# A channel-attention and convolution block of 16 images on one core: the depthwise sums kept in PSUM, the centre tap merged on GpSimd, the LayerNorm tiles copied whole and scaled on GpSimd, a ring of pixel rows, and a new order of the work

## The chip, the cores and the metric

One core of a Trainium2 chip runs the whole program; the other cores are idle. The metric is the device time of one execution in microseconds (us), and of several executions the median. The engines are TensorE (PE, with its weight loads as PEld), VectorE (DVE), ScalarE (ACT), GpSimd (POOL) and SyncE (SP), and 16 DMA engines serve the core. GpSimd issues here the DMAs that add into their target; SyncE issues the plain loads and stores.

## What is computed

The input x is 16 images of 128 channels and 96 by 96 pixels, all fp32. The reference, cut to what matters:

```python
xn1 = _layernorm(x_hwc)                      # over the 128 channels of a pixel
q, k, v = xn1 @ wq.T, xn1 @ wk.T, xn1 @ wv.T # 8 heads of 16 channels
attn = softmax(l2norm(q) @ l2norm(k).T * scale)   # 16 x 16 per head: over channels
x = x + (attn @ v) @ wp.T
xn2 = _layernorm(x_hwc)
h1 = w_in @ xn2                              # 1x1 conv, 128 -> 512 channels
h2 = depthwise 3x3 conv of h1, zero padding  # 512 channels
x = x + w_out @ gelu(h2)                     # 1x1 conv, 512 -> 128 channels
```

The attention is over channels, so it comes down to one 128 by 128 matrix for each image, which the kernel gets from the Gram matrix of the normalised pixels.

## The kernel before

An image is 8 bands of 12 rows (1152 pixels), and a band is 3 units of 4 rows (384 pixels). Channels lie on the 128 partitions. The 512 hidden channels are 4 chunks of 128. The program treats 128 bands, and for each band 4 chunks.

**Normalisation** (`norm`, lines 555 to 754) is done twice for each image, as a (ahead of the attention) and b (behind it). Groups of 4 tiles of 128 pixels are transposed by TensorE into a PSUM bank (`forth`, line 614), so that pixels lie on the partitions. VectorE takes the sums of two tiles at a time (`stats`, 621), GpSimd adds epsilon and raises to the power -1/2 (`variance` 628, `power` 632), VectorE makes the shift for b (636), and ScalarE writes each tile of 128 by 128 scaled, and for b also shifted, into an SBUF buffer zT (668, 672): 4 instructions for a group. In the first image VectorE takes half of these. TensorE forms the Gram matrix from zT (682, a only), and transposes back (719); ScalarE writes the result into the pixel buffers xn (723, 725), each of which holds 24 rows of an image and one more row at either side, so that a row at a border is written twice (729).

**Attention** (757) is a chain of small steps over all engines, once an image. Its result is a matrix that `mix` (571) applies to the normalised pixels; ScalarE writes the product into an x buffer (580), and a DMA of GpSimd's queue adds the image to it (583).

**The convolution** of a chunk goes one of two ways.

- *Job* (`conv_job`, 886): TensorE makes the hidden rows (906), ScalarE copies them from PSUM to SBUF (911; 902 copies the two rows shared with the next band). The nine taps are then summed over shifted windows of these rows. The weights are divided by the centre's, so that the centre is added unscaled. The first tap on VectorE reads two windows in SBUF and writes the sum h3 in SBUF (924); each further one reads a window and h3 and writes h3 (930). Two taps (3 and 5; a third one in chunk 1) are products of ScalarE (919); a DMA of GpSimd's queue adds one product to another (`pr<-pr`, 940), and one more adds the sum to h3 (`h<-pr`, 940). ScalarE takes the gelu in place (944). The windows cut at the image's border have 1140, 1056 or 1045 elements in place of 1152.
- *By matmuls* (`by_matmuls`, 975): chunk 3 of some bands goes directly from xn to the depthwise sum, by nine accumulating matmuls for each unit (990), with the gelu out of PSUM (1000). `PE_BANDS` and `PE_OF` choose these bands: 61 of the 128, which leaves 451 jobs, the last of them without products.

`ffn_out` (1008) multiplies the four gelu results with w_out into PSUM (1017), VectorE adds that to x (1024), and SyncE stores the band.

**PSUM** has 8 banks: 2 for `forth`, 1 for `back`, 1 for the Gram matrix and the attention, and 4 (h) that hidden rows, `mix`, convolutions and outputs share.

**Order.** No engine chooses its work on the chip. `Plan` (58) is a list scheduler that runs while the program is built: each operation has an engine, an assumed duration, what it reads and writes, and a place, which is its turn plus an offset from the table `AT`. The plan goes through an assumed time, lets each engine take the ready operation of the lowest place, and hands out buffers. What comes out is one order, and each engine then works through its own part of it strictly in that order, with semaphores between engines.

Of the kernel before, what the change touches and what calls it, by code (L numbers as in the profile page):

```python
# [20 lines left out]
PE_BANDS = (0, 2, 4, 6, 8, 10, 12)  # L21
PE_OF = 15
# [8 lines left out]
THIRDS = ((1, 1, (0,)),)  # L31
PART, Z_PARTS = 24, 6
QT, QB = 4, 1
H_BANKS = 4
X1_BUFS, XB_BUFS, PR_BUFS, H3_BUFS, ZT_BUFS = 2, 6, 5, 10, 3
IN_TURN = ("tr", "h3", "pr", "xb", "x1")
AT = dict(
    load_w=-20.2, weights=13.4, zeros=-68.05, load_a=-147.85, forth_a=-13.65, stats_a=-60.15, variance_a=574.05,
    power_a=353.05, scaled_a=35.3, gram=0.3, back_a=-44.8, place_a=177.6, attention=-146.15, mix=-16.25,
    residual=204, mixed=-47.8, add_x=-331.2, forth_b=-11.5, stats_b=-104.75, variance_b=68.55, power_b=-326.9,  # L40
    shift_b=-87.05, scaled_b=162.15, back_b=-5.95, place_b=38.15, halo=227.9, hidden=2.75, kept=-114.4,
    products=153.15, add_last=-10.05, tap=4.7, add_first=-147.85, gelu=241.95, conv=3.5, conv_gelu=5.8, out=7,
    add=-70.85, store=278.2, mix_0=-75.3, residual_0=369.55, mixed_0=-142.3, add_x_0=-398.7, gram_0=126.2,
    forth_a_0=-269.2, forth_b_0=-14.9, stats_a_0=-113.85, stats_b_0=-48.05, scaled_a_0=100.95, scaled_b_0=286.6,
    back_a_0=-115.65, back_b_0=-181.55, place_a_0=-352.8, place_b_0=-9.75, shift_b_0=-101.75, late=-3.55,
)
STEP = dict(scaled=0.3, hidden=0.1, products=0.5, tap=0.166, conv=1.6, conv_tap=0.03, out=0.8, out_part=0.05)
# [6 lines left out]
T_POWER = 1000  # L54
T_ADD, T_MOVE = 3060, 1640


class Plan:
# [7 lines left out]
    def __init__(self, **pools):  # L66
        self.free = {p: list(range(n)) for p, n in pools.items()}
        self.slot = {}
        self.ops, self.writer, self.readers, self.users = [], {}, {}, {}
        self.dma = 0.0  # L70
        self.two = 0.0
# [31 lines left out]
    def order(self):  # L103
# [14 lines left out]
        for k, o in enumerate(ops):  # L118
            queues.setdefault(o[0], [])
            idle[o[0]] = True  # L120
            for t in o[5]:
                queue_of[t[0]].append((o[2], k))
# [19 lines left out]
        def dispatch(engine, time):  # L142
# [22 lines left out]
            elif engine == "POOL":  # L165
                rest = self.two - time
                ns, result = (ns, result) if rest <= 0 else (rest + ns - 143, rest + result - 143)
                own = result
            if o[9]:
                self.two = time + ns + 35  # L170
# [42 lines left out]
def tile_restormer_block(  # L213
# [35 lines left out]
    UPP, PARTS = PART // UR, H // PART  # L249
    D = C // HEADS  # L250
    assert PE_CHUNK == NCH - 1 and BR * W >= 8 * P and QT % 2 == 0 and NU * TPU % (QB * QT) == 0 and C == P and UT % P == 0 and H % PART == 0 and PART % BR == 0 and NCH == 4
# [7 lines left out]
    p_tr = ctx.enter_context(tc.tile_pool(name="p_tr", bufs=2, space=PSUM))  # L259
    p_bk = ctx.enter_context(tc.tile_pool(name="p_bk", bufs=1, space=PSUM))  # L260
# [4 lines left out]
    banks = [p_h.tile([P, 4 * P], F32, name=f"h_{k}") for k in range(H_BANKS)]  # L265


    ident = const.tile([P, P], F32, name="ident")
    make_identity(nc, ident)
    blocks = const.tile([P, P], F32, name="blocks")  # L270
# [37 lines left out]
    xns = [pad.tile([P, (PART + 2) * WP + 2], F32, name=f"xn{k}") for k in range(Z_PARTS)]  # L308
# [11 lines left out]

    zT_bufs = [h1p.tile([P, QT, P + 1], F32, name=f"zT_{k}") for k in range(ZT_BUFS)]
# [15 lines left out]
    def part_of(i, r):  # L337

        return (i * PARTS + r // PART) % Z_PARTS, r % PART

    def interior(i, u):
        k, r = part_of(i, u * UR)
        return window(xns[k], r + 1, UR, 1)

    def z_unit(i, u):
        k, r = part_of(i, u * UR)
        return ("z", k, r // UR)
# [754 lines left out]
```

## Time and profile before

| | |
|---|---|
| median of 3 runs | 4148.34 us |
| the runs | 4149.0, 4148.34, 4136.15 us |
| span of the profiled execution (first to last instruction) | 4137.5 us |
| instructions | 52025 |
| moved by DMA | 833.50 MB, mean 201 GB/s |
| HBM read, written | 148.26 MB, 75.50 MB |
| matmuls from xn in `by_matmuls` (two instructions each) | 3294 instructions |
| taps on VectorE | 451 first, 2129 further |
| products on ScalarE | 1028 |

The profile is of one execution. It gives the span but no time of its own beside it, so what lies around the span is seen only against the timed runs: their median is 10.8 us above it. A row of the groups reads: line, engine and operation, the tiles written and read, their shapes, the count, and then the busy time in us, the mean duration of one in ns, and the time that the engine idled just ahead of it. Each fp32 matmul is two instructions, each transpose one. Instructions of one engine overlap a little at their ends, so a mean duration is longer than the time from one start to the next; that time is read from a timeline. The busy share of an engine counts the overlap once.

### The profile page before, as it was taken

How to read it: one execution, taken by the hardware profiler on the slowest of the kernel's cores; microseconds unless marked ns; L12 is line 12 of the kernel's file. 1: busy time of each engine (PE TensorE's matmuls, PEld its weight loads, DVE VectorE, ACT ScalarE, POOL GpSimd, SP SyncE). 2: the span in 40 equal slices, each digit the busy share in tenths (PEclk: the TensorE clock that was granted, in tenths of full speed). 3: DMA queues.
4: the chain of work that ended last, by engine and by line, in shares of the span. 5: the costliest groups of instructions: out<-in, count | busy, mean ns of one | idle time of the engine just before them, and what ended most of it. 6: DMA issues, size and time to landing. Idle time of an engine off the chain costs nothing.

```text
span 4137.5 us, 52025 instructions
## 1 busy us (share of the span) xinstructions
PE 4064.3 (98%) x17217; PEld 2630.9 (64%) x17217; DVE 4048.7 (98%) x4706; ACT 3674.7 (89%) x6993; POOL 2538.1 (61%) x2357
## 2 busy tenths in 40 slices
PE   8999999999999999999999999999999999999999
PEld 6666666666666666666666666666666666666555
DVE  6999999999999999999999999999999999999998
ACT  5899989999889998999899989999889989999886
POOL 4657656566665757657566665666646666566442
PEclk9999999999999999999999999999999999999999
DMA  2999999999999999999999999999999999999998
GB/s 87 193 195 213 205 213 204 206 217 199 211 203 204 209 198 209 216 200 207 199 216 197 209 201 206 213 207 204 200 198 211 205 213 209 194 208 205 192 195 187
DMA packets 205372, 833.50 MB, mean 201 GB/s; under 512 B 23728, under 2 KB 25136, under 8 KB 205104
## 3 DMA queue, kind: packets, MB, share of 16 engines
q0 software_dynamic: 165600, 678.37, 84.6%
q1 hardware_dynamic: 38256, 151.73, 9.8%
q8 instruction: 136, 2.23, 0.2%
q14 instruction: 132, 1.08, 0.1%
q10 hardware_dynamic: 1248, 0.09, 0.0%
HBM read 148.26 MB, written 75.50 MB: 54 GB/s over the span
## 4 chain that ended last, share of the span: by engine, by line
PE 40%; DVE 10%; ACT 5%; DMA 3%; issue 2%; POOL 1%; POOLq 0%; ACTq 0%; DVEq 0%
PE h L990 11%; PE h L1017 10%; PE h L906 8%; DVE h L930 7%; PE g L682 2%; PE h L571 2%; DMA h<-pr 2%; DVE h L924 2%; PE pB_a L719 1%; ACT pr L919 1%; PE pT_b L614 1%; PE pT_a L614 1%; PE pB_b L719 1%; DMA pr<-pr 1%; ACT h L911 1%
## 5 line engine op out<-in xcount | busy, mean ns | idle before, releaser
L930 DVE SCALAR_TENSOR_TENSOR h<-h,ratio,h 128x1140 f32<-128x1140 f32 (+3 forms) x2129 | 2890.9, 1378 | 5.0
L919 ACT ACTIVATE pr<-h,ratio 128x1152 f32<-128x1152 f32 x1028 | 1337.2, 1307 | 98.7 <-DMA h<-pr 63.1
L990 PE MATMUL h<-xn,comp 128*128 128x380 f32 (+1 forms) x3294 | 1160.5, 483 | 3.6 <-ACT h L911 1.5
L1017 PE MATMUL h<-h,woutT 128*128 128x384 f32 x3072 | 1129.9, 487 | 11.4 <-ACT h L944 4.7
L906 PE MATMUL h<-xn,winT 128*128 128x384 f32 (+2 forms) x2706 | 1055.9, 494 | 8.0 <-ACT h L911 6.1
L940 POOL DMA_DIRECT2D pr<-pr x578 | 558.3, 977 | 478.3 <-ACT pr L919 312.0
L990 PEld LDWEIGHTS h<-xn,comp 128*128 128x128 f32 x3294 | 596.9, 190 | 348.8 <-issue 6.5
L911 ACT COPY h<-h 128x384 f32<-128x384 f32 (+2 forms) x1353 | 670.0, 525 | 142.0 <-PE h L906 110.8
L1017 PEld LDWEIGHTS h<-h,woutT 128*128 128x128 f32 x3072 | 555.7, 190 | 347.1 <-issue 25.0
L906 PEld LDWEIGHTS h<-xn,winT 128*128 128x128 f32 x2706 | 485.6, 190 | 302.4 <-issue 35.9
L940 POOL DMA_DIRECT2D h<-pr x450 | 447.6, 998 | 361.5 <-PE h L906 73.8
L924 DVE SCALAR_TENSOR_TENSOR h<-h,ratio 128x1152 f32<-128x1152 f32 x451 | 633.8, 1408 | 5.0 <-ACT h L911 2.8
L944 ACT ACTIVATE h<-h 128x1152 f32<-128x1152 f32 x453 | 549.4, 1216 | 14.9 <-DMA h<-pr 8.9
L632 POOL TENSOR_TENSOR rstd_a<-ve_a,mhalf 128x4 f32<-128x4 f32 x288 | 535.3, 1859 | 13.0 <-POOL ve_a L628 0.2
L628 POOL TENSOR_SCALAR ve_a<-st_a 128x4 f32<-128x4 f32 x288 | 347.3, 1206 | 286.9 <-DVE st_a L621 263.2
L632 POOL TENSOR_TENSOR rstd_b<-ve_b,mhalf 128x4 f32<-128x4 f32 x288 | 516.5, 1794 | 10.6
L672 ACT ACTIVATE zT<-pT_b,nb_b,rstd_b 128x128 f32<-128x128 f32 x1132 | 434.3, 494 | 47.4 <-DVE nb_b L636 40.6
L628 POOL TENSOR_SCALAR ve_b<-st_b 128x4 f32<-128x4 f32 x288 | 285.5, 996 | 301.9 <-DVE st_b L621 285.5
L668 ACT ACTIVATE zT<-pT_a,rstd_a 128x128 f32<-128x128 f32 x1080 | 320.3, 422 | 18.9 <-POOL rstd_a L632 17.7
L682 PEld LDWEIGHTS g<-zT 128*128 128x128 f32 x2304 | 295.1, 192 | 45.0 <-issue 4.4
L682 PE MATMUL g<-zT 128*128 128x129 f32 x2304 | 305.1, 275 | 0.0
L571 PE MATMUL h<-xn,mwT 128*128 128x384 f32 x768 | 287.1, 490 | 6.6 <-ACT h L911 3.2
(171 smaller groups left out, 3585.7 us busy)
## 6 DMA issues: line engine op xcount, KB each, us to landing
pr<-pr POOLq DMA_DIRECT2D x578, 576.0 KB, 7.5
h<-pr POOLq DMA_DIRECT2D x450, 576.0 KB, 7.7
x<-in_x_dram SPq DMA_DIRECT2D x128, 576.0 KB, 6.8
out_dram<-x SPq DMA_DIRECT2D x127, 576.0 KB, 6.3
x<-in_x_dram POOLq DMA_DIRECT2D x122, 576.0 KB, 7.2
out_dram<-x SPq DMA_DIRECT2D x3, 192.0 KB, 1.9
weights<-in_L_conv_w_in_dram SPq DMA_DIRECT2D x1, 256.0 KB, 2.9
weights<-in_L_conv_w_out_dram SPq DMA_DIRECT2D x1, 256.0 KB, 3.0
```

The lines of the kernel that those rows point to most:

```text
L628: nc.gpsimd.tensor_scalar(ve, d["mv"][:, :, 2], 1.0 / C, EPS, ALU.mult, ALU.add)
L632: nc.gpsimd.tensor_tensor(rstd, d["ve"], mhalf, ALU.pow)
L682: nc.tensor.matmul(grams[i][:, : P + 1], lhsT=zt[:, :P], rhs=zt, start=(q == 0 and k == 0), stop=(q == NU * TPU // QT - 1 and k == QT - 1),)
L906: nc.tensor.matmul(rows(ph), lhsT=winT[:, n, :], rhs=window(xn, r0 + r, e - r, 1), start=True, stop=True)
L911: nc.scalar.copy(window(h1_, r, e - r, 1), rows(d.pop(("ph", r))))
L919: nc.scalar.activation(to, shifted(t), AF.Copy, scale=ratio[:, n, t : t + 1])
L924: nc.vector.scalar_tensor_tensor(h3, shifted(t), ratio[:, n, t : t + 1], shifted(UNIT), ALU.mult, ALU.add)
L930: nc.vector.scalar_tensor_tensor(to, shifted(t)[:, lo:hi, cut], ratio[:, n, t : t + 1], to, ALU.mult, ALU.add)
L940: nc.gpsimd.dma_start(out=to, in_=d["pr", t], accum_op=ALU.add)
L944: nc.scalar.activation(h3, h3, AF.Gelu)
L990: nc.tensor.matmul(d["pc"][:, lo:hi, cut], lhsT=comp[:, t, :], rhs=window(xn, r0 + dy, UR, dx)[:, lo:hi, cut], start=(t == order[0]), stop ...
L1017: nc.tensor.matmul(rows(d["po"]), lhsT=woutT[:, n, :], rhs=h3s[g, n][:, s * UR : (s + 1) * UR, :], start=(k == 0), stop=(k == NCH - 1),)
```

## The change

- **Taps.** Every job (but the last) now has three products on ScalarE, taps 3, 5 and a third. GpSimd adds the first of them to the centre's window into one buffer `merged` (both operands in SBUF). VectorE has 5 taps: the first reads a window and `merged`, the middle three read a window and the sum, the last reads a window and the sum and writes h3. The sum `acc` is one buffer in PSUM (3 banks), the same for every job. The other two products are added by DMA, one to the other and then to h3.
- **Bands by matmuls:** 41 in place of 61, so 471 jobs.
- **LayerNorm.** ScalarE copies the PSUM bank of 4 tiles in one instruction to zT; VectorE takes the sums from zT in SBUF; GpSimd scales the four tiles in place with one instruction whose second operand is the 4 columns of the power, broadcast. For b, TensorE multiplies with a centring matrix (identity minus 1/128) in place of a transpose, so the shift goes away. In the first image VectorE scales half.
- **Pixels** lie in one ring of 132 rows, in place of 6 buffers of 24, so a row is written twice only at the ring's seam.
- **PSUM:** `forth` and `back` lose their banks and share the 4 banks h; 3 banks are `acc`.
- **Order:** all offsets of `AT` are new, a `RANK` is added that changes the order but not the turn for a buffer, the plan's idea of VectorE and GpSimd holding each other up is new, and the numbers of buffers change (x 6 to 5, products 5 to 7, h3 10 to 8, zT 3 to 7).

```diff
-PE_BANDS = (0, 2, 4, 6, 8, 10, 12)
-PE_OF = 15
+PE_BANDS = (0, 3, 6, 10, 13, 16, 20, 23, 26)
+PE_OF = 30
-THIRDS = ((1, 1, (0,)),)
+THIRDS = ((0, 1, (0,)), (1, 1, (0,)), (2, 1, (0,)), (3, 1, (0,)))
...
+    acc_banks = p_acc.tile([P, ACC_BANKS * 4 * P], F32, name="acc")
+    acc = acc_banks[:, : BR * W].rearrange("p (r w) -> p r w", w=W)
+    centre = const.tile([P, P], F32, name="centre")
+    nc.vector.tensor_scalar(centre, ident, -1.0 / C, None, ALU.add)
...
-                    nc.tensor.transpose(d["pT", q][:, k, :], xt[:, j * P : (j + 1) * P], ident)
+                    if second:
+                        nc.tensor.matmul(
+                            d["pT", q][:, k, :], lhsT=xt[:, j * P : (j + 1) * P], rhs=centre, start=True, stop=True
+                        )
+                    else:
+                        nc.tensor.transpose(d["pT", q][:, k, :], xt[:, j * P : (j + 1) * P], ident)
...
+                nc.vector.bn_stats(d["st"][:, j, :], zT(qs[h])[:, k : k + 2, :P].rearrange("p t c -> p c t"))
...
+            def copied(q):
+                nc.scalar.copy(zT(q)[:, :, :P], d["pT", q])
+
+            def scaled(engine, q, ks):
+                z = zT(q)[:, ks[0] : ks[-1] + 1, :P]
+                t = (q - qs[0]) * QT
+                rstd = d["rstd"][:, t + ks[0] : t + ks[-1] + 1]
+                engine.tensor_tensor(z, z, rstd.unsqueeze(2).to_broadcast([P, len(ks), P]), ALU.mult)
...
+        def merge():
+            nc.gpsimd.tensor_tensor(merged, d["pr", dma_taps[0]], shifted(UNIT), ALU.add)
...
         def tap(t):
-            h3 = h3_of(g, n)
-            if t == left[0]:
-                nc.vector.scalar_tensor_tensor(
-                    h3, shifted(t), ratio[:, n, t : t + 1], shifted(UNIT), ALU.mult, ALU.add
-                )
+            if t in (left[0], left[-1]):
+                to = h3_of(g, n) if t == left[-1] else acc
+                also = acc if t == left[-1] else merged if dma_taps else shifted(UNIT)
+                nc.vector.scalar_tensor_tensor(to, shifted(t), ratio[:, n, t : t + 1], also, ALU.mult, ALU.add)
                 return
             lo, hi, cut = inside(t, b * BR, BR)
-            to = h3[:, lo:hi, cut]
+            to = acc[:, lo:hi, cut]
             nc.vector.scalar_tensor_tensor(
                 to, shifted(t)[:, lo:hi, cut], ratio[:, n, t : t + 1], to, ALU.mult, ALU.add
             )
...
         def add_products(t):
-            to = d["pr", dma_taps[0]] if t != dma_taps[0] else h3_of(g, n)
-            nc.gpsimd.dma_start(out=to, in_=d["pr", t], accum_op=ALU.add)
+            nc.gpsimd.dma_start(out=d["pr", dma_taps[1]], in_=d["pr", t], accum_op=ALU.add)
+
+        def add_h3():
+            nc.gpsimd.dma_start(out=h3_of(g, n), in_=d["pr", dma_taps[1]], accum_op=ALU.add)
```

More of the change, by code (lines that the diff above doesn't have):

```diff
@@ L164, in dispatch @@
                 result = own = self.dma + result - time
[L165 to L170, printed above, removed]
+            elif engine == "POOL" and o[9]:
+                rest = max(0, self.two - time)
+                ns, result, own = rest + ns, rest + result, rest + own
+                self.held = time + ns
+            if o[9] and engine == "DVE":
+                rest = max(0, self.held - time)
+                ns, result, own = rest + ns, rest + result, rest + own
+                self.two = time + ns
+                self.lost += rest
             push(time + own, "own", k)
@@ L693, in pixels @@
-            op("POOL", T_VARIANCE, at("variance" + ab, s), variance, [], [bt], T_VARIANCE + 33 + SLACK + 200)
-            op("POOL", T_POWER, at("power" + ab, s), power, [], [bt], T_POWER + 33 + SLACK + 700)
-            if second:
-                dve(80, at("shift" + ab, s, i), shift, [], [bt])
-            for h, (q, tr) in enumerate(zip(qs, trs)):
+                zt = zt_of(q)
+                both = [(*zt, j) for j in range(2)]
+                if apart and q % 2 == 0:
+                    four = [(*zt_of(k), j) for k in (q, q + 1) for j in range(2)]
+                    op("POOL", 200, at("zeros", s), lambda q=q: zT(q), [], four, 300)
```

239 lines of the change are left out of this document (129 added, 110 removed).

## The prediction

> **What bounds the kernel now.** First the page's head: the span, the busy shares, and the two DMA queues that carry the traffic (packets, MB, share of 16 engines).
>
> ```profile
> span 4137.5 us, 52025 instructions
> PE 4064.3 (98%) x17217; PEld 2630.9 (64%) x17217; DVE 4048.7 (98%) x4706; ACT 3674.7 (89%) x6993; POOL 2538.1 (61%) x2357
> ...
> q0 software_dynamic: 165600, 678.37, 84.6%
> q1 hardware_dynamic: 38256, 151.73, 9.8%
> ...
> PE 40%; DVE 10%; ACT 5%; DMA 3%; issue 2%; POOL 1%; POOLq 0%; ACTq 0%; DVEq 0%
> ```
>
> Two engines are busy 98% of the time and the DMA engines 94%, so no single one can be sped up alone. The stages tell whether that holds in the middle. A row has the stretch, its length, then for PE, PEld, DVE, ACT and POOL the busy time and (x) the instructions, then the clock, the DMA share and GB/s.
>
> ```profile
> 200.00:4000.00 3800.00, 3753.53 (x15841) 2422.87 (x15840) 3757.68 (x4288) 3442.62 (x6545) 2389.97 (x2154) 1.00 0.97 205
> ```
>
> From 200 to 4000 us VectorE idles for 42 us of 3800, TensorE for about as long, at a full clock. The chain of waits has TensorE with 40% and VectorE with 10% of the span, in pieces of a few us. So the time follows VectorE and TensorE together: it goes down by what the one of them that loses less work loses, as long as ScalarE (89%), GpSimd and the DMA engines don't come up to it. I therefore count each engine's work before and after.
>
> **VectorE, taps.**
>
> ```profile
> L930 DVE SCALAR_TENSOR_TENSOR h<-h,ratio,h 128x1140 f32<-128x1140 f32 x1548 | 2129.6, 1392 | 3.5
> L924 DVE SCALAR_TENSOR_TENSOR h<-h,ratio 128x1152 f32<-128x1152 f32 x451 | 633.8, 1408 | 5.0 <-ACT h L911 2.8 <-PE h L1017 1.5 <-PE pB_a L719 0.6
> L930 DVE SCALAR_TENSOR_TENSOR h<-h,ratio,h 128x1045 f32<-128x1045 f32 x226 | 290.0, 1292 | 0.2
> L636 DVE SCALAR_TENSOR_TENSOR nb_b<-st_b,rstd_b 128x4 f32<-128x4 f32 x288 | 43.4, 151 | 10.0 <-POOL rstd_b L632 9.9
> ```
>
> The means hold overlap, so I take the time from start to start from a timeline (start, duration, engine, what).
>
> ```profile
> 2038.37 0.15 DVE L636 SCALAR_TENSOR_TENSOR nb_b<-st_b,rstd_b 128x4 f32<-128x4 f32 x1
> 2038.44 5.35 DVE L930 SCALAR_TENSOR_TENSOR h<-h,ratio,h 128x1140 f32<-128x1140 f32 x4
> ...
> 2047.67 1.40 DVE L924 SCALAR_TENSOR_TENSOR h<-h,ratio 128x1152 f32<-128x1152 f32 x1
> 2049.11 2.86 DVE L930 SCALAR_TENSOR_TENSOR h<-h,ratio,h 128x1140 f32<-128x1140 f32 x2
> 2051.89 1.41 DVE L924 SCALAR_TENSOR_TENSOR h<-h,ratio 128x1152 f32<-128x1152 f32 x1
> ```
>
> Four taps in 5.35 us, the last of 1.39 whole, give (5.35 - 1.39)/3 = 1.32 us a tap; these are of two jobs in turn. The pair at 2049.11 takes 2.86, so 1.46 from start to start, and it starts 1.44 behind the tap at 2047.67: a tap that waits for the one before it costs 0.11 to 0.14 us more. I take 0.13.
>
> Before there are 451 + 2129 = 2580 taps. After, 471 jobs have 5 each, the last 8: 2358. So 222 fewer, by 1.32: **-293 us**. The 288 shifts of L636 go (0.07 each from start to start, 2038.37 to 2038.44): -20 us.
>
> Now the price of the new form. A tap's sum lies in PSUM. The nearest rows:
>
> ```profile
> L577 DVE SCALAR_TENSOR_TENSOR x<-h,d,x 128x384 f32<-128x384 f32 x18 | 10.8, 612 | 5.1 <-PE h L571 4.9
> L811 DVE TENSOR_TENSOR wide<-g,wqkT 128x256 f32<-128x256 f32 x15 | 6.2, 413 | 4.5 <-ACT wide L807 4.4
> L857 DVE TENSOR_TENSOR em<-e,blocks 128x128 f32<-128x128 f32 x16 | 4.5, 282 | 0.0
> L621 DVE BATCH_NORM_STATS2 st_b<-pT_b 128x6 f32<-128x256 f32 x566 | 234.8, 420 | 8.4 <-PE pT_b L614 7.8
> L1024 DVE TENSOR_TENSOR x<-h,x 128x384 f32<-128x384 f32 x384 | 209.5, 545 | 10.6 <-PE h L1017 10.3
> ```
>
> The taps of 1140 and 1045 elements differ by 100 ns, 1.05 an element. Without that, what is left is 612 - 403 = 209 ns for a form with three operands that reads PSUM (h), 1392 - 1197 = 195 for the tap in SBUF; 413 - 269 = 144 with PSUM (g) against 282 - 134 = 148 without. So reading PSUM costs nothing; that VectorE writes PSUM no row shows. Bounds: half of the 144 ns more or less, 0.07 us by 4 writing taps in 470 jobs, +-132 us. I take 0, as reading does. The statistics, read from SBUF in place of PSUM, I take as unchanged for the same reason.
>
> [...]
>
> There is one sum buffer for all jobs, so each tap waits for the one before it, across jobs too: 470 x 5 = 2350 gaps of 0.13. What hides them is other VectorE work put between: 1152 statistics (566 in the row above) and 384 adds. If every one falls in a gap, 814 stay open (106 us); if none, all do (305). The order is made by a plan that takes any ready work in a gap, so I take 950: **+124 us**.
>
> The first tap still reads two SBUF windows. GpSimd rows show what that means.
>
> ```profile
> 2045.87 0.19 POOL L628 TENSOR_SCALAR ve_b<-st_b 128x4 f32<-128x4 f32 x1 [0.68 <-DVE st_b L621]
> 2047.84 1.29 POOL L628 TENSOR_SCALAR ve_a<-st_a 128x4 f32<-128x4 f32 x1 [1.78 <-DVE st_a L621]
> 2049.09 1.03 POOL L632 TENSOR_TENSOR rstd_b<-ve_b,mhalf 128x4 f32<-128x4 f32 x1
> ```
>
> The read at 2045.87, beside statistics out of PSUM, took 0.19. The same at 2047.84 took 1.29 and ended at 2049.13, just behind the tap of 2047.67 (to 2049.07). So a tap with two SBUF windows holds a GpSimd read up; VectorE work with one does not. That VectorE is held by GpSimd no row shows. A merge can't meet a first tap, since `merged` is one buffer that the tap must have read. A scaling can: 576 of about 1.07 us (below) are 16% of the span, half of one is left on the mean: 470 x 0.16 x 0.5 = 35 us; bounds 0 and three times that, with power and variance counted. I take **+35**.
>
> VectorE: -293 - 20 + 124 + 35 = **-154 us**, 4137.5 to 3983.
>
> **TensorE.**
>
> ```profile
> 2037.67 4.65 PE L990 MATMUL h<-xn,comp 128*128 128x384 f32 x14
> ...
> 2042.16 0.60 PE L614 MATMUL pT_b<-ident,x 128*128 128x128 f32 x4
> ...
> 2070.68 1.05 PE L682 MATMUL g<-zT 128*128 128x129 f32 x8
> ```
>
> From start to start: (4.65 - 0.49)/13 = 0.320 for 384 columns, (0.60 - 0.27)/3 = 0.109 for a transpose, (1.05 - 0.27)/7 = 0.111 for each half of a matmul of 129 columns with its own weights. Bands by matmuls go from 61 to 41, so 1080 of 3294 instructions go: -346. Hidden rows of 20 more jobs, counted over the bands: 170 more of 384 columns, 60 fewer of 480 (0.40 in proportion), 10 more of 288 (0.24): +32. The 1152 transposes of b become matmuls: 0.222 - 0.109 each, +130. **-184 us**, to 3953, if it idles as long as today (4137.5 - 4064.3 = 73). This is below VectorE's 3983, so VectorE is late last, by 30 us.
>
> **ScalarE.**
>
> ```profile
> 2038.66 0.47 ACT L911 COPY h<-h 128x384 f32<-128x384 f32 x1
> 2039.02 1.26 ACT L919 ACTIVATE pr<-h,ratio 128x1152 f32<-128x1152 f32 x1
> 2040.18 1.50 ACT L672 ACTIVATE zT<-pT_b,nb_b,rstd_b 128x128 f32<-128x128 f32 x4
> 2041.55 1.28 ACT L919 ACTIVATE pr<-h,ratio 128x1152 f32<-128x1152 f32 x1
> 2042.69 1.16 ACT L668 ACTIVATE zT<-pT_a,rstd_a 128x128 f32<-128x128 f32 x4
> 2043.69 1.22 ACT L944 ACTIVATE h<-h 128x1152 f32<-128x1152 f32 x1
> 2044.75 0.64 ACT L723 ACTIVATE xn<-pB_b,b 128x384 f32<-128x384 f32 x1
> ```
>
> ```profile
> L919 ACT ACTIVATE pr<-h,ratio 128x1152 f32<-128x1152 f32 x1028 | 1337.2, 1307 | 98.7 <-DMA h<-pr 63.1 <-DMA pr<-pr 33.9 <-ACT xn L725 0.2
> L672 ACT ACTIVATE zT<-pT_b,nb_b,rstd_b 128x128 f32<-128x128 f32 x1132 | 434.3, 494 | 47.4 <-DVE nb_b L636 40.6 <-PE g L682 2.2 <-PE pB_a L719 1.3
> L668 ACT ACTIVATE zT<-pT_a,rstd_a 128x128 f32<-128x128 f32 x1080 | 320.3, 422 | 18.9 <-POOL rstd_a L632 17.7 <-PE g L682 0.7 <-issue 0.2
> ```
>
> From start to start: a hidden copy 0.36, a product 1.16, four scalings 1.37 (b) and 1.00 (a), a gelu 1.06. The 2258 scalings (those of the first image apart, 285 and 279 groups) go: -670. 576 copies of 512 elements come, at 0.47 (128 more elements than a hidden copy, at no more than a product's 1.16/1152 each, make it at most 0.49): +271. Products go from 1028 to 1410: +443. The 20 more gelus are +21, 60 unit gelus of the bands by matmuls go (-24), hidden copies +19, border rows -21, shared rows +10. **+49 us**, 3724: 93% of 3983. It doesn't become the bound, but it has to serve more PSUM banks in time.
>
> **DMA.**
>
> ```profile
> pr<-pr POOLq DMA_DIRECT2D x578, 576.0 KB, 7.5
> h<-pr POOLq DMA_DIRECT2D x450, 576.0 KB, 7.7
> ...
> x<-in_x_dram POOLq DMA_DIRECT2D x122, 576.0 KB, 7.2
> ```
>
> 1028 adds become 470 x 2 = 940, and adds of x 122 become 123: 1063 for 1150, each 0.846 x 4137.5/1150 = 3.04 us of all engines. -264 us: from 94% to 91% of the shorter span.
>
> **GpSimd** gets the work that the others lose.
>
> ```profile
> masks.py:383 POOL TENSOR_SCALAR_AFFINE_SELECT blocks<-blocks 128x128 f32<-128x128 f32 x1 | 0.3, 344 | 0.1
> masks.py:197 POOL MEMSET ident<- 128x128 f32 x1 | 0.2, 204 | 0.3 <-POOLq L1091 0.3
> L648 POOL MEMSET zT<- 128x4 f32 x18 | 0.7, 104 | 0.0
> ...
> L940 POOL DMA_DIRECT2D pr<-pr x578 | 558.3, 977 | 478.3 <-ACT pr L919 312.0 <-DMA pr<-pr 27.4 <-ACT h L911 26.9
> L632 POOL TENSOR_TENSOR rstd_a<-ve_a,mhalf 128x4 f32<-128x4 f32 x288 | 535.3, 1859 | 13.0 <-POOL ve_a L628 0.2
> L628 POOL TENSOR_SCALAR ve_a<-st_a 128x4 f32<-128x4 f32 x288 | 347.3, 1206 | 286.9 <-DVE st_a L621 263.2 <-DVE nb_b L636 16.5 <-DMA pr<-pr 2.5
> ```
>
> No row shows a large two-operand operation. Two memsets of 128 and 4 columns give 0.8 ns an element and 0.1 us fixed; 344 ns for the select give at most 2.7 ns an element, and 1.9 without the fixed part. So a merge of 1152 costs 1.0 to 3.1 us, and I take 1.9 ns: 2.3, with some for the second operand 2.4 us; a scaling of 512 1.07 (0.5 to 1.4). 470 x 2.4 = 1128, 576 x 1.07 = 616, powers 576 x 1.03 and variances 576 x 0.19 = 703, DMA issues 1063 x 0.98 = 1042, the rest 30: 3519 us. The first taps, 470 x 1.33, fill 16% of the span, so of the 1728 reads other than merges 16% meet one and wait 0.7: 194. Together **3713, or 93%** of 3983. Today's 2538 hold nearly 1000 of such waiting (means of 1.86 and 1.2 us where 1.03 and 0.19 are free of it), so there is room, but little is left.
>
> [...] A merge waits for a product of ScalarE and for the first tap of the job ahead; queued behind it are the DMA adds, powers and scalings, and for these wait the gelus, the transposes back and, a job later, VectorE. [...]
>
> **The sum.** VectorE's 3983 in the profiled execution's terms; the median of the timed runs lies 10.8 us above that span: 3983 + 11 = 3994, say **3990** (-3.8%).
>
> **The rivals.**
>
> - *GpSimd is the bound* (slower). At 2.7 ns an element merges take 3.1 us, scalings 1.38: 1775 for the rest + 1457 + 795 + 194 = 4221, with the 89 us that VectorE idles today 4310, + 11 = **4320**. It decides from merges of 2.86 us. For it: VectorE waits for a merge in each job, from a queue that runs in order. Against: the price that the rows suggest is below. 0.14.
> - *The gaps stay open*: all 2350, +181 us on the forecast: **4174**; slower than before from 2150 of them. Against: 1536 pieces of other work. 0.07.
> - *Four banks are too few.* Banks h take 2304 groups of work now, 4 x 4137/2304 = 7.2 us each; after 3625 groups, 4.4 us each, of which (3953 - 73)/3625 = 1.07 is TensorE's writing.
>
> ```profile
> L719 PEld LDWEIGHTS pB_a<-ident,zT 128*128 128x128 f32 x1152 | 144.2, 141 | 110.4 <-issue 42.1 <-ACT xn L725 19.1 <-ACT zT L668 9.2
> ```
>
>   This weight load, behind the one bank of `back`, waits 19.1 us in 384 groups for ScalarE, 0.05 each. If all 3625 groups did: +180 on TensorE's 3953, 4133 + 11 = **4144**. Against: tiles now leave a bank by one copy. 0.08.
> - *Writing PSUM is dear*, at the upper bound: **4122**. [...]
> - *The port isn't freed*: the change's middle taps hold GpSimd's reads up all the same, so 3113 us of taps and 1744 of merges and scalings exclude each other: 4857 + 89 + 11, about **4960**. Against: the read at 2045.87. 0.04.
>
> **How the numbers follow.** The forecast has 0.62, from 3890 (TensorE's 3953, less the 73 us that it idles today, and 11) to 4100. The range 3890 to 4180 takes in the open gaps and the banks, and leaves out GpSimd as the bound (0.14), the port (0.04) and a little below. The measurement can tell 0.3%, 12 us, from no change: faster are the forecast, the dear PSUM and part of the banks, 0.70; within 0.3% the rest of the banks and of the forecast's tail, 0.08; slower 0.22.
>
> **What would show it.** Right: about 1880 taps on `acc` with 1.32 us from start to start, or 1.45 behind their like; merges of 2.2 to 2.6 us beside them; GpSimd 90 to 95% busy, VectorE 95% or more, ScalarE and TensorE 93 to 97%. Wrong: first taps that wait for `merged`; VectorE idle over 150 us; taps of 1.5 us or of several; weight loads that wait for copies; a DMA share above 95%.

## The result, and the profile after

The changed kernel takes **4101.73 us** (median of 4 runs, 4094.66 to 4103.59) where the kernel before took 4142.24 beside it: ratio 0.9905, 95% interval 0.9884 to 0.9926. That is faster by 0.95%, a quarter of the 3.8% forecast (3990), and inside the range. The head of the page after, in the rows shown of before:

```profile
span 4100.5 us, 52124 instructions
PE 3932.9 (96%) x17409; PEld 2600.1 (63%) x17409; DVE 3893.5 (95%) x4170; ACT 3716.6 (91%) x5675; POOL 3492.2 (85%) x3320
...
q0 software_dynamic: 153072, 627.05, 80.3%
q1 hardware_dynamic: 38256, 151.73, 10.2%
...
PE 30%; DVE 25%; POOL 16%; DMA 12%; ACT 10%; issue 7%; POOLq 0%; DVEq 0%; ACTq 0%
```

VectorE's work fell by 155 us (4048.7 to 3893.5) and TensorE's by 131, as the forecast had it for VectorE to within a microsecond. The span fell by 37. The rest is idle time: VectorE 207 us in place of 89, TensorE 168 in place of 73. And the chain of waits is of another kind: TensorE's 40% has become 30%, while VectorE went from 10% to 25%, GpSimd from 1% to 16%, DMA from 3% to 12% and ScalarE from 5% to 10%. (The chain before covers 61% of its span, the one after all of it. Of the part that is covered, TensorE had 66%, VectorE 16%, ScalarE 8%, DMA 5% and GpSimd 2%, so the move from TensorE to GpSimd and DMA is there all the same.) The same stretch as before, in the same columns:

```profile
200.00:4000.00 3800.00, 3653.52 (x16050) 2401.49 (x16050) 3657.55 (x3840) 3520.26 (x5361) 3295.34 (x3061) 0.99 0.93 195
```

Both leading engines idle for 142 to 147 us of 3800 in the middle too, where it was about 42 to 46; it is no matter of start or end. Groups of VectorE after (count, busy, mean ns, idle ahead of them and for what):

```profile
L960 DVE SCALAR_TENSOR_TENSOR acc<-h,ratio,acc 128x1140 f32<-128x1140 f32 x1062 | 1487.0, 1400 | 14.1
L956 DVE SCALAR_TENSOR_TENSOR acc<-h,ratio,merged 128x1152 f32<-128x1152 f32 x470 | 736.9, 1568 | 37.6 <-POOL merged L947 21.8 <-DVE h L956 0.5
L956 DVE SCALAR_TENSOR_TENSOR h<-h,ratio,acc 128x1152 f32<-128x1152 f32 x471 | 661.6, 1405 | 8.4 <-PE h L1065 1.7
L665 DVE BATCH_NORM_STATS2 st_b<-zT 128x6 f32<-128x256 f32 x576 | 244.8, 427 | 31.9 <-ACT zT L690 31.8
L1072 DVE TENSOR_TENSOR x<-h,x 128x384 f32<-128x384 f32 x384 | 211.6, 551 | 53.1 <-PE h L1065 47.8 <-ACT pr L944 2.3 <-ACT xn L745 0.8
```

The middle taps on PSUM cost 1400 ns (1392 in SBUF before) and the last ones 1405: reading and writing PSUM costs next to nothing, 8 ns. Only the first tap, which reads two SBUF windows, is long on the mean, 1568. The idle time is spread over results that come late from everywhere: from TensorE (47.8), ScalarE (31.8) and GpSimd (21.8). Two rows of a timeline show the tap's price. The first tap at 1072.73 takes 1.99 us:

```profile
1071.22 1.41 DVE L956 SCALAR_TENSOR_TENSOR h<-h,ratio,acc 128x1152 f32<-128x1152 f32 x1
1072.73 1.99 DVE L956 SCALAR_TENSOR_TENSOR acc<-h,ratio,merged 128x1152 f32<-128x1152 f32 x1
```

And GpSimd in the same stretch (a span there starts while the instruction ahead of it still runs: the scalings' at 1070.80, with the issue ahead of them ending at 1072.40):

```profile
1067.80 3.76 POOL L947 TENSOR_TENSOR merged<-pr,h 128x1152 f32<-128x1152 f32 x1
1070.18 2.22 POOL L969 DMA_DIRECT2D pr<-pr  x1
1070.80 4.79 POOL L696 TENSOR_TENSOR zT<-zT,rstd_a 128x512 f32<-128x512 f32 x2
1072.80 3.77 POOL L674 TENSOR_TENSOR rstd_a<-ve_a,mhalf 128x4 f32<-128x4 f32 x1
```

So the ends are what can be compared: the merge ends at 1071.56, the DMA issue at 1072.40, the two scalings at 1075.59, the power at 1076.57. From the end of the issue the two scalings take 3.19 us, where two of the shortest (1.04, at 1361.81) would take 2.08. They lose about 1.1 us, just when the first tap runs (1072.73 to 1074.72), and the tap takes 1.99 in place of 1.41. The power ends 0.98 behind the scalings and loses nothing; its 3.77 is a wait in the queue. So in this stretch a tap with two operands in SBUF and GpSimd's scalings, which read SBUF, hold each other up, in both directions: 0.58 us lost by the tap, about 1.1 by the scalings.

Last, ScalarE's waits for sums that the DMA engines form, before and after (us in total, times, longest):

```profile
ACT pr L919 <- DMA h<-pr: 63.1, 65, 3.3
ACT pr L919 <- DMA pr<-pr: 33.9, 35, 2.9
ACT h L944 <- DMA h<-pr: 8.9, 7, 2.4
```

```profile
ACT h L976 <- DMA h<-pr: 54.5, 56, 3.9
ACT pr L944 <- DMA h<-pr: 33.4, 22, 4.3
ACT pr L944 <- DMA pr<-pr: 32.6, 35, 2.8
```

The gelu (L944 before, L976 after) waits for its sum for 54.5 us where it was 8.9.

### The profile page after: what moved, and what is told of

Its sections match the earlier page's. It is cut to its first block, busy times and chain, and to the rows that moved or that the text cites. A ratio compares the mean times of both kernels' runs of the same rounds, so it can differ in the third digit from the quotient of the medians.

```text
span 4100.5 us, 52124 instructions
## 1 busy us (share of the span) xinstructions
PE 3932.9 (96%) x17409; PEld 2600.1 (63%) x17409; DVE 3893.5 (95%) x4170; ACT 3716.6 (91%) x5675; POOL 3492.2 (85%) x3320
## 3 DMA queue, kind: packets, MB, share of 16 engines
q0 software_dynamic: 153072, 627.05, 80.3%
## 4 chain that ended last, share of the span: by engine, by line
PE 30%; DVE 25%; POOL 16%; DMA 12%; ACT 10%; issue 7%; POOLq 0%; DVEq 0%; ACTq 0%
DVE acc L960 12%; PE h L1065 7%; PE h L1037 7%; PE h L928 6%; DMA pr<-pr 5%; DMA h<-pr 5%; DVE acc L956 5%; POOL merged L947 4%; DVE h L956 4%; ACT pr L944 4%; POOL zT L696 3%; PE h L606 2%; PE h L741 2%; PE g L703 2%; PE h L654 2%
## 5 line engine op out<-in xcount | busy, mean ns | idle before, releaser
L960 DVE SCALAR_TENSOR_TENSOR acc<-h,ratio,acc 128x1140 f32<-128x1140 f32 (+2 forms) x1416 | 1948.6, 1376 | 18.5
L944 ACT ACTIVATE pr<-h,ratio 128x1152 f32<-128x1152 f32 x1410 | 1784.1, 1293 | 72.3 <-DMA h<-pr 33.4
L947 POOL TENSOR_TENSOR merged<-pr,h 128x1152 f32<-128x1152 f32 x470 | 1298.6, 2763 | 82.5 <-ACT pr L944 44.0
L928 PE MATMUL h<-xn,winT 128*128 128x384 f32 (+1 forms) x2826 | 1102.6, 495 | 27.9 <-ACT zT L690 10.7
L1037 PE MATMUL h<-xn,comp 128*128 128x380 f32 (+2 forms) x2214 | 805.4, 482 | 2.7 <-ACT h L1047 0.9
L956 DVE SCALAR_TENSOR_TENSOR acc<-h,ratio,merged 128x1152 f32<-128x1152 f32 x470 | 736.9, 1568 | 37.6 <-POOL merged L947 21.8
L972 POOL DMA_DIRECT2D h<-pr x470 | 529.0, 1126 | 236.2 <-DVE h L956 56.8
L956 DVE SCALAR_TENSOR_TENSOR h<-h,ratio,acc 128x1152 f32<-128x1152 f32 x471 | 661.6, 1405 | 8.4 <-PE h L1065 1.7
L969 POOL DMA_DIRECT2D pr<-pr x470 | 548.0, 1174 | 133.2 <-ACT pr L944 98.0
L976 ACT ACTIVATE h<-h 128x1152 f32<-128x1152 f32 (+1 forms) x473 | 563.1, 1191 | 60.9 <-DMA h<-pr 54.5
L696 POOL TENSOR_TENSOR zT<-zT,rstd_a 128x512 f32<-128x512 f32 (+1 forms) x288 | 438.7, 1563 | 4.0
L741 PE MATMUL h<-ident,zT 128*128 128x128 f32 x2304 | 372.0, 277 | 47.7 <-POOL zT L696 34.8
L696 POOL TENSOR_TENSOR zT<-zT,rstd_b 128x512 f32<-128x512 f32 (+1 forms) x288 | 372.3, 1294 | 5.2
```

The source lines that it names most:

```text
L696: engine.tensor_tensor(z, z, rstd.unsqueeze(2).to_broadcast([P, len(ks), P]), ALU.mult)
L741: nc.tensor.transpose(d["pB"][:, j * P : (j + 1) * P], zTs[q][:, k, :P], ident)
L928: nc.tensor.matmul(rows(ph), lhsT=winT[:, n, :], rhs=window(xn, r0 + r, e - r, 1), start=True, stop=True)
L944: nc.scalar.activation(to, shifted(t), AF.Copy, scale=ratio[:, n, t : t + 1])
L947: nc.gpsimd.tensor_tensor(merged, d["pr", dma_taps[0]], shifted(UNIT), ALU.add)
L956: nc.vector.scalar_tensor_tensor(to, shifted(t), ratio[:, n, t : t + 1], also, ALU.mult, ALU.add)
```

## The experiments

Theory *port*: first taps and GpSimd's reads hold each other up, as in the stretch above (0.58 and about 1.1 us), and from GpSimd, which works its queue in order (the power there ends 0.98 us behind the scalings), the delay spreads to all engines. *Port* is only a name for this hold; that the two share a port, no run shows. Rivals: a leading engine's own load is still the bound; four banks are too few; VectorE's wait for `merged` is the cost; the DMA sums land too late; the order is bad. All runs but b1 start from the changed kernel, and where no new order is named they keep its order. The runs that cut something leave out a part of the result; they show what that part costs and are no faster kernels. Each group of runs was made on one chip together with runs of the kernel before, whose median varied from group to group from 4129 to 4143; so the ratios to it are what is compared, and their differences are given in us of 4140. The changed kernel's own interval is 9 us to either side; differences under 12 say nothing.

| run | what differs | median us | ratio [95%] |
|---|---|---|---|
| e1_merge_third | merge of 4 rows | 3999.3 | 0.9672 [0.9654, 0.9689] |
| e2_conv_row | TensorE less | 4096.01 | 0.9905 [0.9877, 0.9933] |
| e3_tap_third | VectorE less | 4088.97 | 0.9885 [0.9867, 0.9902] |
| e6_first_alone | port free, no wait | 4021.14 | 0.9726 [0.9704, 0.9748] |
| e7_centre_direct | port shared, no wait | 4178.1 | 1.01 [1.0083, 1.0118] |
| e8_pointer | port free, wait kept | 4022.75 | 0.9726 [0.9709, 0.9742] |
| e13_third_pointer | e1 and e8 | 3986.04 | 0.965 [0.9636, 0.9665] |
| e14_pointer_conv | e8 and e2 | 4017.95 | 0.9715 [0.9699, 0.9731] |
| e15_pointer_tap | e8 and e3 | 4006.58 | 0.9666 [0.9648, 0.9684] |
| e5_adds_third | DMA sums of 4 rows | 4028.34 | 0.9718 [0.9702, 0.9734] |
| e16_pointer_adds | e8 and e5 | 3959.45 | 0.9552 [0.9537, 0.9567] |
| b1_before_adds | kernel before, DMA sums of 4 rows | 4114.31 | 0.9951 [0.9934, 0.9967] |
| e9_plan_port | new order | 4148.53 | 1.0028 [1.0019, 1.0038] |
| e10_merge_2350 | new order | 4134.84 | 0.9994 [0.9984, 1.0005] |
| e11_order_port_a | new order | 4127.55 | 0.9998 [0.9989, 1.0008] |
| e12_order_port_b | new order | 4112.97 | 0.9962 [0.9947, 0.9976] |
| e17_sum_later | new order | 4128.11 | 0.9979 [0.997, 0.9988] |

**Whose load counts: e1, e2, e3.** The three edits, one in each kernel:

```diff
-nc.gpsimd.tensor_tensor(merged, d["pr", dma_taps[0]], shifted(UNIT), ALU.add)
+nc.gpsimd.tensor_tensor(merged[:, :4, :], d["pr", dma_taps[0]][:, :4, :], shifted(UNIT)[:, :4, :], ALU.add)
...
+            if t != order[0]:        # e2, the convolutions of TensorE
+                hi = lo + 1
...
+            if t == left[1]:         # e3, the second tap of VectorE
+                hi = lo + 4
```

> The changed kernel in its own order, but each merge of GpSimd adds only 4 of the 12 rows (the rest of the merged buffer stays zero, so the output lacks part of the centre and of one tap). This takes about 470 x 1.6 = 750 us from GpSimd's 3492 and nothing from the others. Theory G, that GpSimd's queue is what leaves VectorE and TensorE idle (207 and 168 us): at least 80 us of the 4102 come back, to 4020 or less. Theory B, that four PSUM banks are too few: at most 25 us, 4075 to 4102. Theory O, that every engine is so full that the order breaks everywhere a little: 30 to 60 us.

> The changed kernel in its own order, but eight of the nine matmuls of a convolution on TensorE take one row of the four (those taps are left out elsewhere). That is 984 matmuls by 0.48 us, 470 us less for TensorE, whose groups also leave their PSUM bank earlier. Theory G: at most 30 us come back. Theory B: 80 us or more, since the bank that a convolution holds for 6 us is free after 2. Theory O: 30 to 60 us.

> The changed kernel in its own order, but the second of a job's five taps on VectorE does 4 of its 12 rows (the tap is left out in the rest), 470 x 0.8 = 380 us less for VectorE. If VectorE with its chain on one sum is still the bound, as forecast, 200 us or more come back (to 3900 or less). Theory G: at most 40, since what VectorE waits for comes no sooner. Theory B: at most 60. Theory O: 40 to 100 us.

The page heads of e1, e2 and e3:

```profile
PE 3903.7 (98%) x17409; PEld 2595.8 (65%) x17409; DVE 3843.8 (96%) x4170; ACT 3702.7 (93%) x5675; POOL 2732.3 (68%) x3321
```

```profile
PE 3669.2 (90%) x17409; PEld 2517.6 (61%) x17409; DVE 3893.3 (95%) x4170; ACT 3711.7 (91%) x5675; POOL 3478.5 (85%) x3320
```

```profile
PE 3926.8 (96%) x17409; PEld 2597.4 (64%) x17409; DVE 3588.8 (88%) x4170; ACT 3715.5 (91%) x5675; POOL 3540.4 (87%) x3320
```

264 us off TensorE are worth nothing, 305 off VectorE 8 us; 760 off GpSimd, the least busy of the four, are worth 96. The time doesn't follow the two fullest engines any more. (e2 takes 264 and not the 470 expected: a matmul of 95 columns still shows 271 ns where one of 380 shows 483, and the granted clock was 0.975 where it was 0.994.) What TensorE saves in e2 it waits, above all for GpSimd's scalings, 107.3 us where it was 34.8:

```profile
L741 PE MATMUL h<-ident,zT 128*128 128x128 f32 x2304 | 394.3, 284 | 153.0 <-POOL zT L696 107.3 <-ACT h L933 11.8 <-ACT x L615 9.5
```

e1 also clears the banks of suspicion, as e2 does: with the same four, TensorE reaches 98%.

**The port, or the wait for the merge: e6, e8, e7.** e6 takes `merged` out of the first tap; e8 does too, but reads one element of it as its factor, so it waits as before; e7 adds the centre's window in place of `merged`, so it has two SBUF windows and no wait.

```diff
-                also = acc if t == left[-1] else merged if dma_taps else shifted(UNIT)
+                if t != left[-1]:                                   # e8; e6 with ratio[:, n, t : t + 1]
+                    by = merged[:, 0, 0:1] if dma_taps else ratio[:, n, t : t + 1]
+                    nc.vector.tensor_scalar(to, shifted(t), by, None, ALU.mult)
+                    return
+                also = acc
...
+                also = acc if t == left[-1] else shifted(UNIT)      # e7
```

> The changed kernel in its own order, but the first tap of a job doesn't read the merge: it writes window times ratio (the centre and one tap are left out of the result). So VectorE waits for no merge and no instruction of it reads two SBUF windows; GpSimd still does the merges. Theory G in its narrow form, that the merge and the shared port tie the two engines together: 60 us or more come back, GpSimd's powers and scalings fall to their shortest (1.0 us). Theory B: the 67 us that first taps now take longer than last ones come off VectorE's busy time, but less than 30 us off the whole. Theory O: 20 to 60 us.

> The changed kernel in its own order; the first tap multiplies its window with the first column of the merge in place of the ratio, and adds nothing (the rest of the merge, the centre and one tap are left out of the result). So it waits for the merge just as the changed kernel does, but reads one SBUF window. If the wait was the cost: 4080 or more. If the port was: 4040 or less, first taps of 1.41 us, scalings near 1.4 us.

> The changed kernel in its own order; the first tap reads the centre's window in place of the merge (both in SBUF; the product in the merge is left out of the result). GpSimd makes the merges all the same, and VectorE waits for none of them. So the wait for the merge is gone, and the first tap holds up GpSimd's reads, and they it, as before. If the wait was what cost the 81 us that came back without a merged operand: 4040 or less. If the shared port was: 4080 or more, and GpSimd's scalings of the first normalisation stay near 1.6 us.

e6 and e8 gain the same 74 us: the port costs that, and the wait by itself nothing. e7 loses 81: without the wait the first tap can meet merges too, and it takes 1787 ns on the mean, for 1568 with the wait. So the wait on a single `merged` buffer protects the taps. Groups of GpSimd in the changed kernel, and then in e8:

```profile
L947 POOL TENSOR_TENSOR merged<-pr,h 128x1152 f32<-128x1152 f32 x470 | 1298.6, 2763 | 82.5 <-ACT pr L944 44.0 <-DVE acc L956 29.9 <-ACT zT L690 3.0
L674 POOL TENSOR_TENSOR rstd_a<-ve_a,mhalf 128x4 f32<-128x4 f32 x288 | 437.9, 1624 | 3.7
L696 POOL TENSOR_TENSOR zT<-zT,rstd_a 128x512 f32<-128x512 f32 x270 | 426.1, 1620 | 4.0
```

```profile
L947 POOL TENSOR_TENSOR merged<-pr,h 128x1152 f32<-128x1152 f32 x470 | 1282.6, 2729 | 93.7 <-ACT pr L944 51.3 <-DVE acc L957 28.0 <-DVE acc L964 4.2
L674 POOL TENSOR_TENSOR rstd_a<-ve_a,mhalf 128x4 f32<-128x4 f32 x288 | 386.0, 1411 | 3.7
L696 POOL TENSOR_TENSOR zT<-zT,rstd_a 128x512 f32<-128x512 f32 x270 | 372.8, 1407 | 4.0
```

With the port free, the scalings and powers of a lose 0.21 us each on the mean, those of b 0.04 and 0.05, the merges almost nothing. A few long ones make the difference: the medians of a hardly move (scalings 1357 to 1334 ns, powers 1342 to 1333), while the longest fall from 4624 to 2798 and from 5720 to 2619. The means hold waits in the queue as well, and so in e6 too they did not fall to the 1.0 us expected (1425 ns for both). In e8 GpSimd's busy time is 3367.3, 125 less, and VectorE's 3821.8, 72 less. Who waited for the scalings, in the changed kernel and in e8, is TensorE's transpose back:

```profile
L741 PE MATMUL h<-ident,zT 128*128 128x128 f32 x2304 | 372.0, 277 | 47.7 <-POOL zT L696 34.8 <-ACT x L615 3.2 <-ACT xn L747 3.1
```

```profile
L741 PE MATMUL h<-ident,zT 128*128 128x128 f32 x2304 | 361.5, 274 | 16.1 <-POOL zT L696 9.8 <-ACT x L615 3.4 <-ACT h L1051 0.8
```

**What is late once the port is free: e13, e14, e15.** Each puts the edit of e1, e2 or e3 beside that of e8.

> Both earlier cuts in one kernel: the merge covers 4 of 12 rows, and the first tap takes one SBUF window and a pointer into merged (so the merged part of the sum is left out). Order as in the changed kernel. If the shorter merge (3999 alone) and the freed port (4023 alone) gained by the same thing, the loss at the shared port, the two together give what the better gives, 3985 to 4000, and TensorE stands near 98% of the span. If GpSimd's load costs something of its own beside the port, the two add up, and the time falls under 3970 (4102 less 103 less 79 is 3920).

> The pointer kernel (first tap with one SBUF window, merged part left out) with 8 of 9 convolution matmuls on TensorE cut to one row as well, some 470 us less of TensorE; order as in the changed kernel. Alone the pointer gave 4023 and the shorter convolutions 4096 from 4102. If with the port freed TensorE is what is late next (its share was 97% there), its cut is now worth much more than 6: VectorE's 3823 busy and an idle time of 90 to 150 give 3910 to 3975. If something else holds the rest (GpSimd's load, the order), TensorE's cut is worth under 20 again and it runs 4000 to 4020.

> The pointer kernel with the second tap on 4 of 12 rows as well (part of that tap left out; some 300 us less of VectorE, none of it at the shared port). Order as in the changed kernel. Pointer alone: 4023; TensorE's cut beside it gave 5. If VectorE is what ends last once the port is free, its cut is worth 60 to 110 and TensorE (3904 busy, 97%) becomes the bound: 3925 to 3965. If it isn't, 4005 to 4020, as with the port shared, where the cut gave 13.

The shorter merge and the freed port together give 106 us, not 96 + 74 = 170. Part of the missing 64 may be TensorE's, which stands at 98% there: 170 would end at 3932, below 3959, the shortest time of any run here. But e13 stays 27 above that too, so part of e1's gain was the port's. With the port free the shorter merge still gives 32: GpSimd's load costs something of its own. TensorE's cut is worth 5 (nothing) with the port free, so my guess that TensorE at 97% would be late next was wrong. VectorE's cut of 336 us is worth 25 by the ratios, 16 by the medians: a little, not the bound.

**The DMA's sums: e5, e16, b1.**

```diff
-nc.gpsimd.dma_start(out=d["pr", dma_taps[1]], in_=d["pr", t], accum_op=ALU.add)
+nc.gpsimd.dma_start(out=d["pr", dma_taps[1]][:, :4, :], in_=d["pr", t][:, :4, :], accum_op=ALU.add)
-nc.gpsimd.dma_start(out=h3_of(g, n), in_=d["pr", dma_taps[1]], accum_op=ALU.add)
+nc.gpsimd.dma_start(out=h3_of(g, n)[:, :4, :], in_=d["pr", dma_taps[1]][:, :4, :], accum_op=ALU.add)
```

> The changed kernel with both accumulating DMAs of a chunk on 4 of 12 rows, nothing else cut (most of two products left out of the sum). If the loss is at the port between first taps and GpSimd, 4085 to 4105, and GpSimd's scalings, powers and issues stay as long as they are; if the wait for sums that land late holds the kernel, under 4070.

> The pointer kernel with both accumulating DMAs of a chunk on 4 of 12 rows (most of two products left out of the sum; DMA busy falls by about 35 points of 92%). Order as in the changed kernel. If the DMA's throughput or the time until a sum lands holds the rest, 3975 to 3995; if not, 4010 to 4025. GpSimd's issue instruction may get shorter with the transfer; the profile says by how much, and that part counts for GpSimd.

> The kernel before with its accumulating DMAs of products on 4 of 12 rows (most of those products left out of the sum), nothing else cut; the same cut gave 74 in the changed kernel. If the wait for late sums is new with the change (GELU waited 55 us for them there, 9 here), this gains under 20: 4120 to 4142. If sums that land late held the kernel all along, 4070 or less, and the forecast's cost is not the change's.

e5 is worth 77 us, against the port theory's expectation of nothing. GpSimd's groups stay what they were (scalings 1616, powers 1633, issues 1187 ns), so it isn't GpSimd's time. What moved is the landing, 7.4 us in the changed kernel and 3.4 to 3.5 in e5 (DMA issues: count, KB, us to landing):

```profile
pr<-pr POOLq DMA_DIRECT2D x470, 576.0 KB, 7.4
h<-pr POOLq DMA_DIRECT2D x470, 576.0 KB, 7.4
```

```profile
pr<-pr POOLq DMA_DIRECT2D x470, 192.0 KB, 3.5
h<-pr POOLq DMA_DIRECT2D x470, 192.0 KB, 3.4
```

Loads and stores of x land sooner as well (6.8 to 4.2 us and 5.8 to 3.2), since the cut takes load off the DMA engines (queue q0 from 80.3% to 38.9%); but the waits for them were only 21 us in the changed kernel and are 10 in e5, so the sums are what counts. No run splits how much of a late sum is the transfer's own length and how much the load. This is all that is left in e5 of ScalarE's waits of 54.5, 33.4 and 32.6 us, beside 1.6 and 0.9 in smaller rows:

```profile
ACT pr L944 <- DMA h<-pr: 8.4, 7, 3.2
```

Both cuts together (e16) give 146 us, nearly the sum of 74 and 77: they are two causes, not one. At 3959 it lies below its expected range of 3975 to 3995. In e16 the picture of the forecast comes out: TensorE is late last.

```profile
span 3953.7 us, 52835 instructions
PE 3884.6 (98%) x17409; PEld 2593.5 (66%) x17409; DVE 3812.9 (96%) x4170; ACT 3700.1 (94%) x5675; POOL 3366.5 (85%) x3320
...
PE 65%; ACT 14%; DVE 8%; issue 3%; POOL 2%; DMA 1%; DVEq 0%; ACTq 0%; POOLq 0%
```

In the kernel before the same cut (b1) is worth 20 us, where under 20 was expected, though ScalarE waited 106 us for sums there as well; those waits lay beside a TensorE at 98%. So by this comparison some 57 of the 77 come with the change: the same late sums, no longer hidden. That it is TensorE that hid them is argued from its share, not tested.

**The order: e9, e10, e11, e12, e17.** Everything is computed in these. e9 lets the plan hold variances and powers up at the port too; e10 puts a merge at 2350 ns in place of 2400; e11 and e12 are e9 with offsets searched anew; e17 lets the plan expect GpSimd's DMAs 1 us later.

```diff
-            pool(T_POWER, at("power" + ab, s), power, [], [bt])
+            pool(T_POWER, at("power" + ab, s), power, [], [bt], True)      # e9, e11, e12, variance too
-T_MERGE = 2400
+T_MERGE = 2350                                                             # e10
-WAIT = dict(POOL=350, SP=1300, ACT=1300)
+WAIT = dict(POOL=1350, SP=1300, ACT=1300)                                  # e17
```

> The changed kernel with another order: the plan is told that GpSimd's variances and powers too are held up by a first tap and hold it up, as the trace shows; in the changed kernel it knows this of merges and scalings only. All instructions stay. The offsets were chosen for the other plan. If the order counts most (it broke because the plan's picture was wrong), at least 20 us come back, to 4080 or less; if the port costs what it costs in any order, 4085 to 4120; if the offsets fit only the plan for which they were chosen, 4120 or more.

> The changed kernel with another order: the plan takes 2.35 us for a merge in place of 2.40, and nothing else changes. This says how much of the changed kernel's 4102 hangs on that one order. If an order chosen for one set of numbers is worth as much on the chip as in the plan, this one, for which the offsets weren't chosen, is 30 us slower or more (4130 and up); if what holds the chip's execution back blurs that, it lies within 15 us of 4102.

> The changed kernel with a new order and nothing else, everything computed: the variances and powers are also planned as held while VectorE's first tap runs, and the offsets of the order were searched again under that plan, whose own end is 4010 (it was 4049 with the old offsets, which ran 4149: 99 more than planned). If the plan now sees what costs, the gap stays near 99 and this runs 4090 to 4115, about what the changed kernel runs. If an order can avoid the collisions at the port, it falls to 4020 to 4060. If the plan still misses what matters, it is slower than 4120.

> As the run before, from another start of the search: the plan's own end is 4014. Expected 4090 to 4120 if the plan's gap of 99 stays, 4020 to 4060 if the order avoids the port, over 4120 if the plan misses what matters; a spread of more than 20 between the two orders, whose planned ends differ by 4, would say that the order moves the time by more than the plan can tell.

> The changed kernel, everything computed, with one number of its plan changed: the plan takes it that a DMA started by GpSimd lands 1 us later, so that GELUs and the reuse of product buffers are placed later; its own end goes from 3962 to 4004. If an order that reckons with late sums cures that wait, GELU's wait for sums falls under 20 us and the time to 4040 to 4080. If the order's scatter is larger than what the plan gains (five orders so far ran from 4102 to 4149), 4095 to 4150.

None beats the changed kernel: the six orders run from 4102 to 4149. A change of 50 ns in one assumed duration moves the time by 37 us by the ratios (e10). In e17 the gelu's wait for sums does fall, to 24.1 us, but other waits take its place (the first tap's for `merged` is 38.1), so this didn't cure it. No version here that computes everything gains from what was learnt.

## Why the prediction was wrong

- **VectorE, work: right by luck, by two errors that cancel.** 3983 less 89 idle is 3894, and 3893.5 is measured. In it the port's share was **+35** and measures 72 (e8: 3821.8). So the other terms together are some 37 too high; no row tells which, the open gaps with their +124 are the likeliest. The taps are as forecast: 470 + 1416 on `acc`, 2.86 us for two in a row as before, PSUM free.
- **VectorE, idle: the step that failed.** The sum took it that VectorE would idle for 89 us as it does now, with the cover of a time that "follows VectorE and TensorE together". It idles for 207, and the miss in the span, 4100.5 - 3983 = 118, is all there: 207 - 89.
- **Why it idles: GpSimd's hold.** The forecast counted GpSimd's 194 us of holding as busy time that fits (93%). It stayed lower, 3492, of which 125 goes when the port is free; but it does not need to be full to be late (85% busy, and e1's cut of it is worth 96 us). The nearly 1000 us of waiting that it read from the spans before count some time twice, since spans overlap: GpSimd's groups there add up to 2835 us, in 2538 of busy time. And the forecast had no term for what waits behind a held instruction in the queue. Port: 74 us of time, by e6 and e8.
- **Why it idles: the DMA.** "91% of the shorter span" was right (90.5%), but the forecast had no term for the time until a sum lands. The sums land in 7.4 us, as before (7.5 and 7.7), and every job needs two in a row, as before (there, chunk 1 even three). Late they cost 77 us, by e5; the same cut was worth 20 before (b1). New ahead of them in the queue are merges and scalings; no run shows how much that adds.
- **TensorE, ScalarE:** forecast 4064.3 - 184 = 3880 and 3724 busy, measured 3933 (3885 in e16) and 3717. The 3953 that TensorE's work would allow is the 3953.7 of e16, where TensorE idles 69 us for the 73 assumed.
- **GpSimd's prices:** 2.4 us for a merge is the shortest one (2408 ns; median 2695), 1.07 for a scaling is near the 1.03 and 1.04 us of short ones (at 1031.51 and 1361.81).
- **Rivals.** Dear PSUM (chance 0.05; middle taps of 1400 ns for 1392 in SBUF), four banks (e2: 264 us off TensorE are worth nothing) and port not freed (4960 us, for 4102): each refuted. *GpSimd is the bound* was nearest in its place and wrong in its condition: merges of 2.86 us weren't reached (2.76 on the mean, waits in the queue included), and yet its load counts (e1). The *gaps stay open* case would have put 181 us on VectorE's work, which came out as forecast. The + 11 around the span was scatter of the runs of before: here 4102.16 of the profiled execution lies 1.7 above its span.
- **Of the signs named,** "VectorE idle over 150 us" and "first taps that wait for `merged`" came, the first as a symptom of both causes, the second harmless (e8).

What stays open: at the port two things end at once in e6 and e8, the hold of VectorE (72 us) and that of GpSimd (125). e3 and e15 speak against VectorE's load as the way the price is paid, and e1, e2 and the transposes that wait for scalings speak for GpSimd's. But in e7 VectorE's busy time grows by 99 us and the time by 81, so its own hold is not ruled out; no run splits them. How much of the loss a better order could win back is open too.

## What to carry to other kernels

When two engines share all the time, work moved to a third is not free because that engine has room: ask how many results an in-order queue now has to deliver on time, and how long the way from one result to the next engine is. Add up idle time as a term of its own; here the busy sums of VectorE, TensorE and ScalarE came within 1.4% and the idle time was the miss. Here a VectorE operation with two operands in SBUF, beside a GpSimd that reads SBUF, cost both, 74 us in all. The taps with one operand in PSUM didn't show that cost (1400 ns), and the wait on `merged` kept taps and merges apart (first taps of 1568 ns, 1787 without it); these are two ways to try.

## What the hardware showed that was not expected

- GpSimd's instructions that only start a DMA have shorter spans when the port is free, on the mean: 1174 to 1068 and 1126 to 1042 ns. But their medians stay (927 to 921, and 921 in both), and only the longest fall (4222 to 2330, 4157 to 2492). A span holds the wait behind a held instruction too, so it isn't shown that an issue itself is held.
- A single operand that comes as a column per partition is not seen to meet GpSimd at the port: the first tap of e8 takes 1412 ns on the mean and at most 1462, like those on PSUM (1400 and 1405 on the mean).
- A first tap without its wait can take 8.76 us (e7, the longest; 4.07 in the changed kernel). The spans of merges don't show such meetings: the longest is 5.84 in e7 and 6.03 in the changed kernel, where the wait keeps merge and tap apart, so a long span there is a wait in the queue.
